# A gated block with attention on one core: features in rows for the last layer, the output projection and the result; statistics in pairs at the start; the last gates computed in one step with their scale

## The chip, the cores and the metric

The kernel runs on one core of a Trainium2 chip. The metric is device time in microseconds of one execution. The core has five engines that run their own queues of instructions in order: TensorE (PE, with its weight loads shown apart as PEld), VectorE (DVE), ScalarE (ACT), GpSimd (POOL) and SyncE (SP, which here only issues DMAs). They meet through semaphores. TensorE writes to PSUM, which this kernel divides into eight banks of 128 x 512 float32.

## The reference

Eight sequences of 512 tokens with 256 features, all float32. A layer norm feeds two branches, whose product is added to the input:

```python
x = L0_attn_query                      # (8, 512, 256)
xn = _layernorm(x, axis=-1)
s = _L0_attn_ref(xn, in_proj_w, out_proj_w)   # 16 heads of 16, rope, causal window of 250
g = _silu(_L0_ffn_ref(xn, k0, k1, k2, s0, s1, s2))
x = x + s * g
return x
```

The feed-forward branch has three layers (512 to 1024, 1024 to 1024, 1024 to 256), the first of which sees `[xn, -xn]`. Its kernels are boolean and stand for +1 and -1; each layer has one scale, and the first two end in `2 * relu`.

## The kernel before

**Precision.** Activations of the feed-forward branch are split into a float16 high part and a rest that is fed as fp32r; both are multiplied with the same +1/-1 weights, kept in both types (`w0`, `w1`, `w2` with `h` and `l`). So each product of this branch is a pass over `h` and a pass over `l`, summed in one PSUM bank. The attention's projections are float32.

**Stages of a batch b.** `stats` and `norm` make xn with tokens in rows; `turn_x` transposes it on PE (`xnT_ps`, L268) into `xT` (features in rows), and into its high and low parts. `project` makes the two halves `a` and `b` (the two members of each rope pair) of k and of q: DVE multiplies each with cos and sin (`m_ka`, `m_kb`, `m_qa`, `m_qb`, L319), POOL adds (`rotate`, L339), ACT and DVE split the result (`split_hi` L356, `split_lo` L363), and it goes through DRAM into stacks of four heads. `project_v` makes v. `layer` (L415) makes `h1` (eight tiles of 128 features by 512 tokens) and `h2` (eight more); after each, ACT writes the high part (L426) and DVE the low part (L424). `last` makes z, the third layer, and the gate: before, with **tokens** in rows, 128 tokens by 256 features per tile `t` of four: the stationary operand is a piece of h2, the moving one is w2. `gate_ready` makes silu out of it: exp on ACT (L496), plus one on POOL (L499), reciprocal on DVE (L503), and a product on POOL (L504). Attention goes in nine score steps per batch (`step`): scores (L605), exp (L624), masks on POOL (L640, L647), values (L679), `keep` (L699, L703), and the division by the sums (`invert`, `divide`). `project_o` (L782) multiplies with w_o, again 128 tokens by 256 features per tile; DVE multiplies with the gate (L804), POOL adds the residual, which `project_o` has loaded from `x` again (L787, L809), and SP stores (L810).

**What sets the order.** The order on all five queues is written by a planner in the code. Each piece has a due place (`at`) and a PE cost; pieces are sorted by `at`, their costs add up to a clock, and a piece may name follow-up work with a delay on that clock. A batch has `SEQ = 42` units of `at`; `last_at` places the z of batch b among the h1 tiles of batch b+1, `late` places its output projections. Score steps are put before those pieces that are in `quick`, evenly by cost. Batch 0 starts at -40: loads, statistics, transposes, `warm` blocks (matmuls of the identity), the weights (`make_w0`, `make_w1`, on DVE, ACT and POOL), then k, q, h1 and v. In the last batch layer 2 runs in two halves of 256 tokens; z of tiles 0 and 1 follows the first half (`how == "soon"`), z of tiles 2 and 3 the second (`"final"`).

**Buffers.** PSUM: two tiles of two banks for scores (`ps_s`), one bank for the values (`ps_o`), three single banks (`ps_m`, tag `mm`) for everything else: transposes, projections, h, z, output projection. `m_*b` has one buffer, so the rope products of q's b half wait for k's rotation. SBUF tags that matter here: `gate0` to `gate3` (single), `den` and `xr` (two each, 128 x 256), `xn` (two).

**Loads at the start.** SP issues x tiles 0 and 1, k0, rope, k2, w_o; ACT issues x tiles 2 and 3, the scales, w_qkv (one load, L124) and k1 (L127).

Of the kernel before, what the change touches and what calls it, by code (L numbers as in the profile page):

```python
# [21 lines left out]
EPS = 1e-5  # L22
# [12 lines left out]
def tile_attention_times_gated_ffn(  # L35
    ctx: ExitStack,
    tc: tile.TileContext,
    x: bass.AP,
    w_qkv: bass.AP,
# [6 lines left out]
    out: bass.AP,  # L46
):

# [75 lines left out]
    nc.scalar.dma_start(wqkv_sb, w_qkv.rearrange("(c p) f -> p c f", p=P))  # L124
# [44 lines left out]
    def make_w0(c):  # L169

        nc.vector.tensor_tensor(w0["h"][:, c], kb0[:, c], kb0[:, EC + c], ALU.subtract)
        nc.scalar.copy(w0["l"][:, c], w0["h"][:, c])
# [58 lines left out]
    def stats(b):  # L231
        st = states[b] = {}
        mv = small.tile([P, NT, 2], F32, tag="mv", name=f"mv_{b}")
        rstd = small.tile([P, NT], F32, tag="rstd", name=f"rstd_{b}")
        for t in range(NT):
            bn = small.tile([P, 6], F32, tag="bn", name=f"bn_{b}_{t}")
            nc.vector.bn_stats(bn, xs[b, t])
            nc.vector.bn_aggr(mv[:, t, :], bn)
        nc.vector.tensor_scalar(rstd, mv[:, :, 1], EPS, None, ALU.add)
        nc.gpsimd.tensor_tensor(rstd, rstd, minus_half, ALU.pow)  # L240
        nc.vector.scalar_tensor_tensor(
            mv[:, :, 1], mv[:, :, 1], LEAST_VAR, ones, ALU.is_ge, ALU.mult,
            accum_out=counts[:, 2 * B + b : 2 * B + b + 1],
        )
        st["mv"], st["rstd"] = mv, rstd
# [9 lines left out]
    def turn_x(b, t, plain=False):  # L255
# [10 lines left out]
        pt = ps_m.tile([P, EC, P], F32, tag="mm", name=f"xnT_ps_{b}_{t}")  # L266
# [7 lines left out]

        def parts_():
            xT = st["xT"][:, :, ts(t, P)]
            if b == 0:
                nc.scalar.copy(xT, pt)
            else:
                nc.vector.tensor_copy(xT, pt)  # L280
            nc.scalar.mul(hi, pt, sgnx)
# [3 lines left out]

        return [(0.0, parts_), (0.5, low)]

# [14 lines left out]
    def project(b, what, part):  # L302
        st = states[b]
        col = E * "qk".index(what) + P * "ab".index(part)
        ps = ps_m.tile([P, T], F32, tag="mm", name=f"{what}{part}_ps_{b}")
# [11 lines left out]

        def times(i):
            nc.vector.tensor_tensor(  # L319
                m[:, i], ps, rope_sb[:, i if part == "a" else 1 - i], ALU.mult  # L320
            )

        def both():
            times(0)
            times(1)
            if part == "b":
                return [
                    (1.4, lambda: rotate(b, what)),
                    (4.0 if b else 7.0, lambda: split_hi(b, what)),
                    (5.1 if b else 8.2, lambda: split_lo(b, what)),  # L330
                ]

        return [(0.0, both)]
# [95 lines left out]
    def last(b, t, how):  # L429
        st = states[b]  # L430
        pz = ps_m.tile([P, E], F32, tag="mm", name=f"z_ps_{b}_{t}")
        if how == "at once":
            for c in range(NF1):
                nc.tensor.matmul(
                    pz, st["h2p"][:, c, ts(t, P)], w2["l"][:, c].bitcast(F32),
                    start=(c == 0), stop=(c == NF1 - 1),
                )
        else:
            for p in "hl":
                for c in range(NF1):  # L440
                    nc.tensor.matmul(  # L441
                        pz, st["h2" + p][:, c, ts(t, P)], w2[p][:, c],
                        start=(c == 0 and p == "h"), stop=(c == NF1 - 1 and p == "l"),
                    )
        gate = st["gate", t] = outs.tile([P, E], F32, tag=f"gate{t}", name=f"gate_{b}_{t}")
        if how == "final":
            den = denominator(b, t)

            def ends():
                nc.scalar.activation(den, pz, AF.Exp, scale=scales[:, 1:2])  # L450
                nc.vector.tensor_scalar(gate, pz, scales[:, 0:1], None, ALU.mult)
                return [(0.3, add)]

            def add():
                nc.scalar.activation(den, den, AF.Identity, bias=1.0)
                return [(0.3, invert_)]

            def invert_():
                nc.vector.reciprocal(den, den)
                if t + 1 < NT:  # L460
                    nc.gpsimd.tensor_tensor(gate, gate, den, ALU.mult)
                st["den"] = den
# [3 lines left out]
        def scale():  # L466
            nc.vector.tensor_scalar(gate, pz, scales[:, 0:1], None, ALU.mult)
            if how != "later":
                return [(0.5 if t == 0 else 4.5, lambda: gate_ready(b, t))]
# [20 lines left out]
    def denominator(b, t):  # L490
        return work.tile([P, E], F32, tag="den", name=f"den_{b}_{t}")

    def gate_ready(b, t):
        st = states[b]
        gate, den = st["gate", t], denominator(b, t)
        nc.scalar.activation(den, gate, AF.Exp, scale=-1.0)  # L496

        def add():
            nc.gpsimd.tensor_scalar(den, den, 1.0, None, ALU.add)  # L499
            return [(0.9, invert_)]  # L500

        def invert_():
            nc.vector.reciprocal(den, den)  # L503
            return [(1.8, lambda: nc.gpsimd.tensor_tensor(gate, gate, den, ALU.mult))]  # L504
# [7 lines left out]
    def last_at(b, t):  # L512

        if b + 1 < B:
            return SEQ * (b + 1) + 2 * L1 * (t + 1) + L3 * t
        half = t // 2
        return SEQ * b + NF0 * L1 + NT * L3 + HALF * (half + 1) - 2 * L3 + L3 * (t % 2)

    def late(b, t):

        if b + 1 == B and t >= NT // 2:
            return last_at(b, NT - 1) + L3 + 0.9 * (t - NT // 2)
        if b + 1 == B:
            return SEQ * b + 40.0 + 0.9 * t
        return SEQ * (b + 1) + (32.0 + 3.2 * t if b + 2 < B else 18.0 + 2.5 * t)

    def finish_ffn(b, t, how):
        quick.add(last_at(b, t))
        out = [(last_at(b, t), L3, lambda: last(b, t, how))]
        if how == "later":  # L530
            out.append((late(b, t) - 4.0, 0, lambda: gate_ready(b, t)))
        return out

    def ffn(b):
# [3 lines left out]
        for f in range(NF0):  # L538
# [3 lines left out]
            if f % 2 and b > 0:  # L542
                now += L3
# [234 lines left out]
    def project_o(b, t, final=False):  # L778
        st = states[b]
        pp = ps_m.tile([P, E], F32, tag="mm", name=f"att_ps_{b}_{t}")  # L780
        for c in range(EC):
            nc.tensor.matmul(  # L782
                pp, st["V", c][:, ts(t, P)], wo_sb[:, c, :],
                start=(c == 0), stop=(c == EC - 1),
            )
        xr = work.tile([P, E], F32, tag="xr", name=f"xr_{b}_{t}")
        nc.sync.dma_start(xr, x[b, ts(t, P), :])  # L787
        st["xr", t] = xr
        if final and t + 1 == NT:
            att = work.tile([P, E], F32, tag="xn", name=f"att_{b}_{t}")  # L790

            def out_of_psum():
                y, den = st["gate", t], st["den"]
                nc.scalar.copy(att, pp)
                nc.gpsimd.tensor_tensor(y, y, att, ALU.mult)
                nc.vector.tensor_tensor(y, y, den, ALU.mult)
                nc.vector.tensor_tensor(y, y, xr, ALU.add)
                nc.sync.dma_start(out[b, ts(t, P), :], y)
# [3 lines left out]
        def product():  # L802
            y = st["gate", t]
            nc.vector.tensor_tensor(y, pp, y, ALU.mult)  # L804
            return [(1.0 if final else 0.5, store)]

        def store():
            y = st.pop(("gate", t))
            nc.gpsimd.tensor_tensor(y, y, xr, ALU.add)  # L809
            nc.sync.dma_start(out[b, ts(t, P), :], y)  # L810
# [3 lines left out]
    def finish(b, final=False):  # L814
        out = []
        for t in range(NT):
            end = final and t >= NT // 2
            out.append((late(b, t), 0.87, lambda t=t, end=end: project_o(b, t, end)))
# [25 lines left out]
    def swap():  # L844
# [5 lines left out]
        (-38.5, 0, signs), (-40.5, 0, lambda: warm(12)), (-34.5, 0, lambda: warm(3)),  # L850
        (-32.5, 0, lambda: warm(5)),
        (19.2, 0, make_w2), (22.5, 0, swap), (SEQ * (B - 1) + 45.0, 0, add_up),
    ]
    for c in range(EC):
        everything.append((-30 + 0.1 * c, 0, lambda c=c: make_w0(c)))
# [9 lines left out]
    for b in range(B):  # L865
        everything += prepare(b) + ffn(b)
        for t in range(NT):
            how = "later" if b + 1 < B else "soon" if t < NT // 2 else "final"
            everything += finish_ffn(b, t, how)
# [59 lines left out]
    with tc.If(found < n_rows):  # L929
        for b in range(B):  # L930
# [4 lines left out]
            for t in range(NT):  # L935
                run(finish_ffn(b, t, "at once"))
# [67 lines left out]
```

## Time and profile before

| | us |
|---|---|
| median of three runs | 627.94 (627.25 to 629.54) |
| profiled execution, its time | 628.36 |
| its span, first to last instruction | 626.6 |
| PE busy | 608.6 |
| DVE busy | 394.1 |
| POOL busy | 316.2 |
| ACT busy | 299.7 |

The span lies 1.8 us inside the time of the same execution. Busy times of engines overlap. A line of the timeline has the start (us from the span's start), the duration of the merged group, the engine, the line of the kernel, the operation, the tiles written and read, the shapes, the count, and in brackets the idle time of the engine just before it with what ended it. A line of the list of waits has the waiting engine, tile and line, what it waited for, the microseconds in total, the number of times and the longest. Groups by line and shape that come up later:

```
L424 DVE h2l   512 columns x56: 680 ns     256 columns x16: 398 ns
L426 ACT h1h   512 columns: 597 ns         L496 ACT exp, 256 columns: 409 ns
L499 POOL +1   256 columns: 852 ns         L767 POOL tensor_scalar, 512 columns: 1499 ns
L503 DVE reciprocal, 256 columns: 1752 ns  L754 DVE reciprocal, 128 columns: 933 ns
L504 POOL product, 256 columns: 755 ns     L763 POOL product, 512 columns: 1285 ns
L804 DVE product out of PSUM, 256 columns: 403 ns
L809 POOL add of the residual, 256 columns: 810 ns
```

DMA issues to landing: w_qkv 8.0 us (768 KB), k0 8.2 (512 KB), rope 9.9 (512 KB), k1 11.3 (1024 KB, landed at 15.04), residual 2.8 (128 KB), store of the result 1.7 (128 KB).

### The profile page before, as it was taken

What the parts mean: (1) busy time and instruction counts of PE and PEld (TensorE: products, weight loads), DVE (VectorE), ACT (ScalarE), POOL (GpSimd) and SP (SyncE); (2) the same over time, 40 slices, a digit from 0 to 9 for tenths busy, and PEclk for the clock granted to TensorE, in tenths of its full rate; (3) what the DMA queues carried; (4) which work ended last, traced back from release to release, by engine and by line L of the source; (5) the groups of instructions that cost most, each with busy time, mean ns of one, the idle gap of its engine ahead of it and who ended that gap; (6) DMA issues with size and microseconds to landing.
All of it is one profiled execution on the core that took longest, in us unless ns stands there. A gap on an engine that the chain in (4) does not pass through costs nothing.

```text
span 626.6 us, 12051 instructions
## 1 busy us (share of the span) xinstructions
PE 608.6 (97%) x4842; PEld 398.4 (64%) x4842; DVE 394.1 (63%) x667; ACT 299.7 (48%) x441; POOL 316.2 (50%) x409
## 2 busy tenths in 40 slices
PE   8899999999999999999999999999999999999994
PEld 6455576556665567655676566765676556767793
DVE  6773535667575774766658576485665668456573
ACT  4566655534554445545354454453444544564411
POOL 2954542456533655427634366235662356638641
PEclk9999999999999999999999999999999999999998
DMA  9352721116311263114421252412532116230101
GB/s 273 117 197 95 260 85 51 51 68 216 122 51 51 87 208 110 52 51 172 139 93 51 75 214 76 143 33 86 208 94 88 51 69 227 77 109 19 53 18 48
DMA packets 38193, 67.20 MB, mean 107 GB/s; under 512 B 5104, under 2 KB 19184, under 8 KB 38128
## 3 DMA queue, kind: packets, MB, share of 16 engines
q1 hardware_dynamic: 36384, 64.24, 30.5%
q10 hardware_dynamic: 1744, 2.10, 1.0%
q8 instruction: 40, 0.66, 0.4%
q14 instruction: 25, 0.20, 0.1%
HBM read 36.96 MB, written 29.36 MB: 106 GB/s over the span
## 4 chain that ended last, share of the span: by engine, by line
PE 85%; DVE 5%; POOL 3%; DMA 3%; ACT 2%; issue 1%; SPq 0%; POOLq 0%; ACTq 0%; DVEq 0%
PE h_ps L415 41%; PE po L679 11%; PE z_ps L441 9%; PE sc L605 8%; PE v_ps L292 4%; PE att_ps L782 4%; PE qa_ps L307 2%; PE kb_ps L307 2%; PE qb_ps L307 2%; DMA kb<-in_k_dram 2%; PE ka_ps L307 2%; PE xnT_ps L268 1%; DVE den L503 1%; DVE h2l L424 1%; DVE xn L250 1%
## 5 line engine op out<-in xcount | busy, mean ns | idle before, releaser
L624 ACT ACTIVATE p<-sc 128x1024 f32<-128x1024 f32 (+2 forms) x144 | 138.5, 1013 | 75.0 <-PE sc L605 41.0
L415 PE MATMUL h_ps<-h1l,w1l_sb 128*128 128x512 f32 (+1 forms) x576 | 144.2, 392 | 0.0
L640 POOL TENSOR_SCALAR_AFFINE_SELECT p<-p 128x512 f32<-128x512 f32 x128 | 90.3, 711 | 104.0 <-ACT p L624 104.0
L415 PE MATMUL h_ps<-h1h,w1h_sb 128*128 128x512 f16 (+1 forms) x576 | 123.0, 356 | 0.5 <-ACT v_pad L299 0.5
L415 PEld LDWEIGHTS h_ps<-h1l,w1l_sb 128*128 128x128 f32 x576 | 99.5, 188 | 25.7 <-issue 6.8
L426 ACT ACTIVATE h2h<-h_ps 128x512 f16<-128x512 f32 (+1 forms) x72 | 39.6, 550 | 140.3 <-PE h_ps L415 140.2
L415 PEld LDWEIGHTS <-w1h_sb 128*128 128x128 f16 x576 | 51.5, 98 | 55.1 <-issue 13.4
L679 PE MATMUL po<-p,v_pad 128*32 128x378 f32 (+4 forms) x1216 | 77.2, 372 | 1.3 <-DVE S L703 1.1
L647 POOL TENSOR_SCALAR_AFFINE_SELECT p<-p 128x512 f32<-128x512 f32 (+1 forms) x96 | 50.0, 521 | 54.6 <-ACT p L624 49.7
L424 DVE SCALAR_TENSOR_TENSOR h2l<-h_ps,h2h 128x512 fp32r<-128x512 f32 (+1 forms) x72 | 44.3, 617 | 48.5 <-ACT h2h L426 48.5
L503 DVE RECIPROCAL den<-den 128x256 f32<-128x256 f32 x30 | 52.5, 1752 | 28.2 <-POOL den L499 28.1
L424 DVE SCALAR_TENSOR_TENSOR h1l<-h_ps,h1h 128x512 fp32r<-128x512 f32 x64 | 42.4, 675 | 34.8 <-ACT h1h L426 34.8
L605 PEld LDWEIGHTS sc<-q,k 32*128 32x128 f32 x1216 | 44.1, 184 | 26.1 <-issue 15.0
L754 DVE RECIPROCAL S<-S 128x128 f32<-128x128 f32 x64 | 58.9, 933 | 0.0
L426 ACT ACTIVATE h1h<-h_ps 128x512 f16<-128x512 f32 x64 | 38.2, 597 | 41.8 <-PE h_ps L415 41.2
L605 PE MATMUL sc<-q,k 32*128 32x378 f32 (+4 forms) x1216 | 57.2, 306 | 0.0
L415 PE MATMUL h_ps<-xl,w0l_sb 128*128 128x512 f32 x128 | 52.5, 491 | 0.0
L679 PEld LDWEIGHTS po<-p,v_pad 128*32 128x32 f32 x1216 | 31.3, 109 | 30.8 <-issue 16.2
L809 POOL TENSOR_TENSOR gate<-gate,xr 128x256 f32<-128x256 f32 x31 | 25.1, 810 | 46.8 <-DMA xr<-in_x_dram 41.2
L441 PE MATMUL z_ps<-w2l_sb,h2l 128*128 128x256 f32 x256 | 38.3, 291 | 0.4 <-DVE h2l L424 0.4
L415 PE MATMUL h_ps<-xh,w0h_sb 128*128 128x512 f16 x128 | 38.6, 383 | 0.0
L339 POOL TENSOR_TENSOR m_ka<-m_ka,m_kb 128x512 f32<-128x512 f32 x16 | 20.1, 1278 | 30.3 <-DVE m_kb L319 30.3
(97 smaller groups left out, 811.0 us busy)
## 6 DMA issues: line engine op xcount, KB each, us to landing
q<-dq SPq DMA_DIRECT2D x64, 256.0 KB, 3.6
dq<-qh SPq DMA_DIRECT2D x16, 512.0 KB, 3.4
dq<-m_qa SPq DMA_DIRECT2D x16, 512.0 KB, 5.0
k<-dk SPq DMA_DIRECT2D x32, 256.0 KB, 2.8
dk<-kh SPq DMA_DIRECT2D x8, 512.0 KB, 2.6
dk<-m_ka SPq DMA_DIRECT2D x8, 512.0 KB, 2.6
xr<-in_x_dram SPq DMA_DIRECT2D x32, 128.0 KB, 2.8
out_dram<-gate SPq DMA_DIRECT2D x32, 128.0 KB, 1.7
```

Of the source, the lines that this page charges most:

```text
L307: nc.tensor.matmul(ps, wqkv_sb[:, c, ds(col, P)], st["xT"][:, c, :], start=(c == 0), stop=(c == EC - 1),)
L415: nc.tensor.matmul(ph, w[p][:, c, ts(f, P)], st[src + p][:, c, cols], start=(k == 0), stop=(k == n - 1),)
L424: nc.vector.scalar_tensor_tensor(lo, ph, 0.0, hi, ALU.max, ALU.subtract)
L426: high = lambda: nc.scalar.activation(hi, ph, AF.Relu)
L441: nc.tensor.matmul(pz, st["h2" + p][:, c, ts(t, P)], w2[p][:, c], start=(c == 0 and p == "h"), stop=(c == NF1 - 1 and p == "l"),)
L503: nc.vector.reciprocal(den, den)
L605: nc.tensor.matmul(sc[r // 2][:, r % 2, ds(off, n)], st["k0", g][row, ts(j, P)], st[f"q{turn}", g][row, ds(j * P + first, n)], start=(turn ...
L624: nc.scalar.activation(p[:, 2 * half : 2 * half + 2, :n], sc[half][:, :, :n], AF.Exp, scale=D ** -0.5,)
L640: nc.gpsimd.affine_select(out=block, in_=block, compare_op=ALU.is_ge, fill=0.0, base=0, pattern=[[0, 4], [1, P]], channel_multiplier=-1,)
L647: nc.gpsimd.affine_select(out=block, in_=block, compare_op=ALU.is_ge, fill=0.0, base=-1, pattern=[[0, 4], [-1, beyond]], channel_multiplier=1,
L679: nc.tensor.matmul(po[32 * r : 32 * r + 32, ds(j * P + first, n)], v_columns(j, g, r), p_[:, r, ds(off, n)], start=(j == 0), stop=(done an ...
L754: nc.vector.reciprocal(part, part)
```

## The change

1. **Features in rows.** `last`, `project_o` and the result are turned: w2 and w_o are now the stationary operands, h2 and V the moving ones. A batch's z has two units `u` of 128 features by 512 tokens instead of four tiles of 128 tokens by 256 features; in the last batch four units of 128 features by 256 tokens. The residual comes from a transposed copy of x, the result is written transposed (`x_t`, `out_t`), and both are laid out on the host. `residual` is issued in `gate_ready` or `last`, ahead of the projection, not in it. `den` and `xr` are single buffers (`beside`). The reciprocal of `gate_ready` is cut into two halves. Places change (`last_at`, `late`): z comes after the fourth and the eighth tile of h1, not after every second.
2. **The start.** w_qkv is loaded in three parts, k's first. The deviations of batch 0 are made in pairs of tiles. Transposes of tiles 0 and 1 and the projections of q use the score pool. The high and low parts of x come after all four copies. `w0h` of the first half is placed ahead of them on DVE. The `warm` blocks are 9, 2 and 1 matmuls, where they were 12, 3 and 5. The products of q's b half come 1.5 units later.
3. **The last batch.** All four projections come after the last z, whose banks are from the score pool. The gate of the last two units is one operation, z times scale times reciprocal, and the last store is issued by ACT.

```diff
-    nc.scalar.dma_start(wqkv_sb, w_qkv.rearrange("(c p) f -> p c f", p=P))
+    for n in (1, 0, 2):
+        nc.scalar.dma_start(
+            wqkv_sb[:, :, ts(n, E)], w_qkv[:, ts(n, E)].rearrange("(c p) f -> p c f", p=P)
+        )
...
+            if (t + 1) % n == 0:
+                part = rstd[:, t + 1 - n : t + 1]
+                nc.vector.tensor_scalar(part, mv[:, t + 1 - n : t + 1, 1], EPS, None, ALU.add)
+                nc.gpsimd.tensor_tensor(part, part, minus_half[:, :n], ALU.pow)
...
+        if b == 0:
+
+            nc.scalar.copy(xT, pt)
+            st["parts", t] = [high, low]
+            if t + 1 == NT:
+                first_parts(2, 3)
+            return
...
+        if b == 0 and what == "q":
+            ps = ps_s.tile([P, 2, T], F32, tag="sc", name=f"{what}{part}_ps_{b}")[:, 0]
...
-        return [(0.0, both)]
+
+        return [(1.5 if b == 0 and what + part == "qb" else 0.0, both)]
...
+    def outputs(b):
+
+        n = 1 if b + 1 < B else 2
+        return [(f, ts(half, T // n)) for half in range(n) for f in range(EC)]
...
+    def residual(b, u):
+        f, cols = outputs(b)[u]
+        xr = states[b]["xr", u] = beside(b, u, "xr")
+        nc.sync.dma_start(xr, x_t[b, ts(f, P), cols])
...
-                        pz, st["h2" + p][:, c, ts(t, P)], w2[p][:, c],
+                        pz, w2[p][:, c, ts(f, P)], st["h2" + p][:, c, cols],
...
+                nc.scalar.activation(den, den, AF.Identity, bias=1.0)
+                return [(0.0 if u == 2 else 0.88, ready)]
...
+            def ready():
                 nc.vector.reciprocal(den, den)
-                if t + 1 < NT:
-                    nc.gpsimd.tensor_tensor(gate, gate, den, ALU.mult)
-                st["den"] = den
+                nc.vector.scalar_tensor_tensor(
+                    gate, pz, scales[:, 0:1], den, ALU.mult, ALU.mult
+                )
...
+            return [(0.9 + 1.1 * k, lambda k=k: invert_(k)) for k in range(2)]
...
         if b + 1 < B:
-            return SEQ * (b + 1) + 2 * L1 * (t + 1) + L3 * t
+            return SEQ * (b + 1) + 4 * L1 * (u + 1) + 2 * L3 * u
...
         if b + 1 == B:
-            return SEQ * b + 40.0 + 0.9 * t
-        return SEQ * (b + 1) + (32.0 + 3.2 * t if b + 2 < B else 18.0 + 2.5 * t)
+            return last_at(b, 3) + L3 + 0.9 * u
+        return SEQ * (b + 1) + (33.5 + 6.4 * u if b + 2 < B else 19.2 + 5.0 * u)
...
-                pp, st["V", c][:, ts(t, P)], wo_sb[:, c, :],
+                pp, wo_sb[:, c, ts(f, P)], st["V", c][:, cols],
...
+            very_last = final and u + 1 == len(outputs(b))
+            adder, queue = (nc.vector, nc.scalar) if very_last else (nc.gpsimd, nc.sync)
+            adder.tensor_tensor(y, y, xr, ALU.add)
+            queue.dma_start(out_t[b, ts(f, P), cols], y)
...
-        (-38.5, 0, signs), (-40.5, 0, lambda: warm(12)), (-34.5, 0, lambda: warm(3)),
-        (-32.5, 0, lambda: warm(5)),
+        (-34.6, 0, signs), (-40.5, 0, lambda: warm(9)), (-34.7, 0, lambda: warm(2)),
+        (-32.5, 0, lambda: warm(1)), (-31.0, 0, lambda: enough(0)),
+        (-32.7, 0, lambda: first_parts(0, 1)),
...
-        everything.append((-30 + 0.1 * c, 0, lambda c=c: make_w0(c)))
+        everything += [
+            (-34.4 if c == 0 else -32.8, 0, lambda c=c: make_w0h(c)),
+            (-32.9 if c == 0 else -32.6, 0, lambda c=c: make_w0l(c)),
+        ]
```

## The prediction

> **What bounds the kernel now.** I read the stretch-by-stretch busy times first, because the page's averages (PE 97%, DVE 63%) mix stages with different limits:
>
> ```profile
> core 0: us, PE busy (x) PEld busy (x) DVE busy (x) ACT busy (x) POOL busy (x), PEclk, DMA share, GB/s
> 0.00:11.00 11.00, 8.00 (x48) 7.48 (x49) 6.49 (x24) 3.95 (x9) 3.12 (x10) 1.00 0.82 253
> 11.00:18.00 7.00, 7.00 (x19) 2.93 (x18) 6.01 (x10) 4.46 (x4) 2.77 (x3) 1.00 0.82 240
> 18.00:34.00 16.00, 12.65 (x53) 7.45 (x52) 11.88 (x24) 8.87 (x15) 14.63 (x11) 1.00 0.37 145
> ...
> 116.00:190.00 74.00, 73.89 (x581) 47.30 (x579) 47.97 (x80) 34.62 (x51) 37.24 (x49) 1.00 0.32 108
> ...
> 560.00:616.00 56.00, 54.48 (x548) 45.85 (x541) 34.59 (x60) 19.82 (x37) 31.40 (x40) 1.00 0.16 48
> 616.00:626.60 10.60, 1.46 (x7) 0.95 (x5) 4.09 (x6) 1.10 (x3) 2.29 (x3) 0.76 0.12 34
> ```
>
> The reader should see that the middle is PE alone (73.89 of 74 us), so nothing done there to another engine shortens the kernel. Time can be won before 34 us, in the last batch, and after its last matmul. The timeline of the start says what PE waits for there:
>
> ```profile
> 6.26 1.05 POOL L240 TENSOR_TENSOR rstd<-rstd,minus_half 128x4 f32<-128x4 f32 x1 [3.56 <-DVE rstd L239]
> 7.35 0.73 DVE L250 TENSOR_SCALAR xn<-x,mv,rstd 128x256 f32<-128x256 f32 x2 [0.17 <-POOL rstd L240]
> ...
> 15.23 2.38 POOL L180 TENSOR_SCALAR w1l_sb<-kb,sgn,sgnn 128x1024 fp32r<-128x1024 uint8 x2 [7.92 <-DMA kb<-in_k_dram]
> ...
> 17.57 2.51 POOL L339 TENSOR_TENSOR m_ka<-m_ka,m_kb 128x512 f32<-128x512 f32 x2
> ...
> 20.12 1.29 DVE L319 TENSOR_TENSOR m_qb<-qb_ps,rope_sb 128x512 f32<-128x512 f32 x2 [2.18 <-POOL m_ka L339]
> ...
> 21.46 1.13 PE L292 MATMUL v_ps<-wqkv_sb,xT 128*128 128x256 f32 x4 [1.32 <-DVE m_qb L319]
> ```
>
> A chain runs from a load (k1, landed at 15.04) over two weight conversions on POOL and the rotation of k to the rope product of q (DVE, 20.12), and from there to PE. Further PE waits of 0.76, 0.80 and 0.46 us follow at 27.85, 31.60 and 33.19. In the list of waits two lines concern what the change enlarges or moves:
>
> ```profile
> POOL gate L809 <- DMA xr<-in_x_dram: 41.2, 19, 3.4
> ...
> DVE den L503 <- POOL den L499: 28.1, 24, 2.5
> ```
>
> The first is the residual, loaded only when it is wanted; the second is DVE held at a reciprocal until POOL has added 1. Neither shows as PE time in the middle. Last I read the tail, after the last matmul:
>
> ```profile
> 616.92 1.74 DVE L459 RECIPROCAL den<-den 128x256 f32<-128x256 f32 x1
> ...
> 618.86 0.41 DVE L796 TENSOR_TENSOR gate<-gate,den 128x256 f32<-128x256 f32 x1
> ...
> 619.30 0.83 DVE L797 TENSOR_TENSOR gate<-gate,xr 128x256 f32<-128x256 f32 x1
> 620.16 0.35 SPq L798 DMA_DIRECT2D out_dram<-gate  x1
> 620.61 1.14 SPq L810 DMA_DIRECT2D out_dram<-gate  x1
> ```
>
> [...] (1) [...] 16 matmuls of z (256 columns) take 1.83 us in the chain of waits, 16 of layer 2 (512 columns) 3.6 to 3.8. (2) [...] DVE stood 2.18 us before m_qb, with h1l, whose input was ready, behind it. (3) [...] the h2l operation takes 398 ns at 256 columns and 680 at 512.
>
> **The change, part by part.** All sums are made against the profiled execution: span 626.6, time 628.36, which is 0.42 above the median of 627.94.
>
> *Features in rows, middle of the kernel.* Per batch z goes from 64 matmuls of 256 columns to 32 of 512, the output projection from 16 instructions to 8. Columns are the same; [...] and over seven batches **-0.7** (bounds -1.2 and +0.5: the chain's rows do not separate 2 x 1.83 from 3.6 to 3.8). DVE, ACT and POOL get fewer, larger pieces: POOL goes from 4 x (0.85 + 0.75 + 0.81) = 9.6 us per batch to about 2 x (1.5 + 1.28 + 1.28) = 8.1 (512-column rows of L767 and L763). PE's queue covers this, so I cost it at nothing. The residual is issued 4.5 planner units before its use instead of beside it, so the 41.2 us of POOL waits go; PE did not see them, so they are worth nothing either. Its buffer is now single, so on SP the second residual load waits for the first half's final add; behind it stand k/q stores and loads, for which the old store waited the same way. The per-gate chain becomes longer: exp 0.6, add 1.5, two reciprocals 3.5, product 1.3 = 6.9 us, where it was 0.41 + 0.85 + 1.75 + 0.75 = 3.8. The plan leaves it 4.5 units and the projection's 1.75, plus a score step if one falls in between. DVE will therefore sometimes stand before the product. I place z, v and h1 of the next batch by hand on the three PSUM buffers: h1l of the first tile frees its bank about 3.5 us after that tile began, the third h1 wants one at 3.6. This just fits: 0; if it slips, it is the slower rival.
>
> *The start.* x's deviations in pairs: pow runs at about 5.2 and 6.45 instead of once at 6.26; the first normalization comes at 6.35, not 7.35, the third at 7.5. Four copies on ACT (0.38 each), now without the f16 parts between them, end near 9.2, and the last warm block is one matmul, not five. w_qkv was one load, landed at about 10.2 (8.0 us from issue); its k third is now first, by my estimate from 253 GB/s there by 7. So ka starts at 9.25, not 11.06. But this is not the gain. On DVE w0h0 now stands ahead of all four xl, waits for k0 (landed about 9.9), and DVE then has 2 x 1.2 + 4 x 0.45 + 0.25 to do before m_ka: 14.4 instead of 13.16; m_kb ends at 17.0. The rotation of k cannot start before 15.04 + 0.2 + 2.38 = 17.6 in either kernel. Three ACT issues of about 0.5 us stand where one was, ahead of k1's, so k1 may land 0 to 1 us later. What does gain: q's banks come from the score pool, free when xl of tiles 0 and 1 are done (13.7 and 14.1), so qa, qb, h1_0, h1_1, v0 run 13.75, 15.5, 17.2, 18.1, 19.0, and h1l0 (19.0) passes ahead of m_qb, which still waits until 20.1. At 21.4 PE has v0 and h1_2 done, where v0 just started before. h1l1 and h1l2 follow m_qb, so the low part of k starts at 22.8, not 25.09, and the rest of the DVE queue (h1l3 to h1l7, statistics of batch 1) moves up by the same 2.3: layer 2 starts at about 30.9, not 33.19. I take **-2.0** (bounds -3.0 and -0.5: each 0.1 us of k1 delay costs 0.1).
>
> *The last batch, before its end.* PE waits 1.11 us at 572.99 for keep (DVE), behind the reciprocal of batch 6's gate, and 0.41 at 592.03, where z waits for h2l behind a count. In the new order that h2l precedes the count (0.41 goes), and the first wait keeps most of its length, since the two half reciprocals and the 1.5 us add take its place. **-0.5** (bounds -1.2 and +0.5).
>
> *The tail.* All four projections come after the last z, so z ends 2 x 0.86 = 1.72 us sooner (614.0, not 615.74) and PE ends where it did. DVE then decides: reciprocal of gate 2 at 613.25 to 615.0, joined gate 0.45, product 0 0.41, reciprocal of gate 3 615.95 to 617.7, joined gate to 618.15, the add of output 1 to 618.6, product 3 to 619.0, last add 0.41 to 0.83: the last store is issued at 619.5 to 619.9, now on ACT, where it was 620.61 on SP. **-0.9** (bounds -1.3 and 0). The price is DVE order: without the joined gate two more DVE operations would stand here.
>
> Sum: -0.7 - 2.0 - 0.5 - 0.9 = -4.1; 628.36 - 4.1 = 624.3, or **623.8** against the median.
>
> **Rivals.** *The start stays pinned to k1.* If k1 lands 1 us later, or m_kb is pushed past it (0.6 us of slack), the start gives 0.8, z nothing, the last batch 0.3, the tail 0.7: -1.8, 626.1. For it: POOL idled 7.92 us for that load, and "k sooner" does not touch it. Against: the bytes ahead of k1 are the same.
>
> *Bursts of h1.* Four tiles of h1 now come together between the z blocks, with ACT 0.60 and DVE 0.69 for each 0.91 of PE, and three v beside them. A loss of 0.4 per batch in seven batches gives -4.1 + 2.8 = -1.3, 626.6. Against: PE idles only 0.1 us per batch there now.
>
> *The wide gate chain (slower).* At the border of two batches DVE holds, in order, the second product, h2l, two keeps, count and h1l0. If the gate is over 0.5 us later than I placed it, every later one of these slips and PE waits for a bank. A slip of 1.2 us beyond that in seven batches is +8.4, in all +4.3: 632.2. For it: 28.1 us of DVE waits on the same add, soon 1.5 us long instead of 0.85, and a chain of 6.9 us in some 6.3 to 8. Against: those waits cost PE nothing now, and POOL has 1.5 us less to do per batch and no residual to wait for.
>
> **Chances.** About 0.5% (3.1 us) is what a measurement of this kernel can tell from no change. Forecast 0.64 (0.58 of it beyond 0.5%), k1 0.17 (0.02 beyond), bursts 0.09 (none), gate chain 0.10 (0.09 slower by over 0.5%). Faster 0.60, same 0.31, slower 0.09. The range, 621.5 to 627.5, takes the start's and tail's outer bounds and both middle cases, and leaves out the gate chain and the extremes.
>
> **What would show it.** Right: ka at about 9.3, the rotation of k still at 17.6, low k near 22.8, layer 2 near 31; 73.9 of 74 us of PE busy in the middle and a batch period not longer than the present 75; the last store issued 0.7 to 1.1 us sooner relative to the end of PE. Wrong: k1 landing after 15.5, PE waiting at the head of a batch for h1l or the product, or a last reciprocal that starts after 616.5 on the shifted scale.

## The result and the profile after

The changed kernel takes 623.75 us (median of five runs, 621.87 to 624.11), the kernel before, measured beside it, 628.63 (627.25 to 629.54): a ratio of 0.9916, 95% interval 0.99 to 0.9931. The forecast was 623.8. Its parts, however, were not of the sizes forecast. This table is read from the two profiled executions:

| us | before | after | difference |
|---|---|---|---|
| k1 landed | 15.04 | 15.43 | +0.39 |
| layer 2 of batch 0 starts | 33.19 | 32.36 | -0.83 |
| first h1 of batch 1 | 87.99 | 87.17 | -0.82 |
| batch period, mean of six (first h1 of batch 1 to that of batch 7) | 74.985 | 74.630 | -0.355, six times: -2.13 |
| last batch: its first h1 to the end of PE | 79.56 | 78.61 | -0.95 |
| end of PE to the end of the span | 9.10 | 7.50 | -1.60 |
| span | 626.56 | 621.05 | -5.51 |
| time of that execution | 628.36 | 623.75 | -4.61 |

What lies outside the span grew from 1.8 to 2.7 us in these two executions (1.9 to 2.3 in the other four of the changed kernel), so the spans differ by more than the times. The stretch-by-stretch busy times of the changed kernel (start and end, length, then busy time and count of PE, PEld, DVE, ACT and POOL, the granted clock, the DMA share and rate):

```profile
9.00:18.00 9.00, 8.75 (x24) 4.21 (x25) 7.45 (x14) 6.31 (x10) 2.39 (x3) 1.00 0.86 262
18.00:31.00 13.00, 9.15 (x38) 5.37 (x37) 10.99 (x21) 7.40 (x13) 12.80 (x11) 1.00 0.40 157
116.00:190.00 74.00, 73.95 (x543) 44.16 (x542) 46.91 (x76) 35.64 (x50) 35.57 (x44) 1.00 0.32 107
558.00:614.00 56.00, 54.32 (x546) 44.41 (x542) 36.44 (x60) 20.96 (x38) 30.34 (x35) 1.00 0.15 45
614.00:621.10 7.10, 0.00 (x0) 0.00 (x0) 1.33 (x4) 0.00 (x0) 1.00 (x2) 0.83 0.23 73
```

The middle is PE alone, as before (73.95 of 74 us, with 543 matmuls in place of 581). The stretch from 18 to 31 us is still not: PE idles 3.9 of 13 us while POOL is full. The timeline of the start says why:

```profile
15.61 2.38 POOL L188 TENSOR_SCALAR w1l_sb<-kb,sgn,sgnn 128x1024 fp32r<-128x1024 uint8 x2 [8.44 <-DMA kb<-in_k_dram]
...
17.95 2.50 POOL L381 TENSOR_TENSOR m_ka<-m_ka,m_kb 128x512 f32<-128x512 f32 x2
...
20.49 1.29 DVE L360 TENSOR_TENSOR m_qb<-qb_ps,rope_sb 128x512 f32<-128x512 f32 x2 [1.47 <-POOL m_ka L381]
...
22.43 1.13 PE L328 MATMUL v_ps<-wqkv_sb,xT 128*128 128x256 f32 x4 [1.38 <-DVE h1l L466]
...
22.78 2.50 POOL L381 TENSOR_TENSOR m_qa<-m_qa,m_qb 128x512 f32<-128x512 f32 x2
22.90 3.47 DVE L405 TENSOR_TENSOR m_ka<-m_ka,kh 128x1024 fp32r<-128x1024 f32 x1
...
27.02 1.13 PE L328 MATMUL v_ps<-wqkv_sb,xT 128*128 128x256 f32 x4 [1.64 <-DVE h1l L466]
...
29.94 0.16 DVE L260 SCALAR_TENSOR_TENSOR mv<-mv,ones 128x4 f32<-128x4 f32 x1
...
32.36 1.89 PE L457 MATMUL h_ps<-h1h,w1h_sb 128*128 128x512 f16 x8 [0.46 <-ACT v_pad L335]
```

The chain of before is whole: k1, two conversions, k's rotation, q's rope product. Low k (`m_ka<-m_ka,kh`, the low part of k) starts at 22.90 instead of 25.09, but lasts 3.47 us instead of 2.11, beside POOL's rotation of q: it ends at 26.36, only 0.83 sooner. From there DVE's queue runs as before, and layer 2 follows 5.99 us later in both kernels, so this 0.83 is what layer 2 gained. In the list of waits (us in total, times, longest) these lines stand in the place of the two that the prediction named:

```profile
DVE den L572 <- POOL den L567: 25.2, 15, 2.9
...
POOL gate L882 <- DVE gate L875: 12.1, 9, 4.9
...
POOL gate L574 <- DMA xr<-in_x_t_dram: 11.1, 4, 2.8
```

The wait for the added 1 was 28.1 us (24 times). The add of the residual (now L882) waited 41.2 us for its load; it now waits for DVE's product alone. The 11.1 us that are still put down to that load stand before the gate's product (L574), which does not read it. PE waits for none of them in the middle. The timeline after the last matmul, which ends at 613.55:

```profile
611.91 1.74 DVE L528 RECIPROCAL den<-den 128x256 f32<-128x256 f32 x1
...
613.68 0.48 DVE L529 SCALAR_TENSOR_TENSOR gate<-z_ps,scales,den 128x256 f32<-128x256 f32 x1
614.08 0.41 DVE L868 TENSOR_TENSOR gate<-gate,xr 128x256 f32<-128x256 f32 x1
...
614.42 0.41 DVE L875 TENSOR_TENSOR gate<-att_ps,gate 128x256 f32<-128x256 f32 x1
...
614.87 0.50 DVE L882 TENSOR_TENSOR gate<-gate,xr 128x256 f32<-128x256 f32 x1
615.40 0.37 ACTq L883 DMA_DIRECT2D out_dram<-gate  x1
```

The last store is issued 1.85 us after the end of PE, where it was 3.15 (620.61 against 617.46). The other 0.3 us of the tail lies between issue and the end of the span; it is not to be read, since from the end of PE to the end of the span it was 7.0 to 7.5 us in the runs below that leave the tail as it is.

### The profile page after: what moved, and what is told of

The parts are those of the page before. It is cut to its first block, busy times and chain, and to the rows that moved or that the text cites. A ratio compares the mean times of both kernels' runs of the same rounds, so it can differ in the third digit from the quotient of the medians.

```text
span 621.1 us, 11288 instructions
## 1 busy us (share of the span) xinstructions
PE 604.3 (97%) x4546; PEld 372.5 (60%) x4546; DVE 382.9 (62%) x641; ACT 299.7 (48%) x428; POOL 308.1 (50%) x367
## 4 chain that ended last, share of the span: by engine, by line
PE 90%; DVE 3%; DMA 2%; POOL 2%; ACT 1%; issue 0%; ACTq 0%; POOLq 0%; DVEq 0%
PE h_ps L457 45%; PE po L746 11%; PE z_ps L511 9%; PE sc L672 8%; PE v_ps L328 4%; PE att_ps L853 4%; PE qa_ps L346 2%; PE kb_ps L346 2%; PE qb_ps L346 2%; DMA kb<-in_k_dram 2%; PE ka_ps L346 2%; PE xnT_ps L291 1%; ACT p L691 1%; DVE den L528 1%; DVE m_ka L405 1%; DMA x<-in_x_dram 1%
## 5 line engine op out<-in xcount | busy, mean ns | idle before, releaser
L707 POOL TENSOR_SCALAR_AFFINE_SELECT p<-p 128x512 f32<-128x512 f32 x128 | 92.3, 727 | 133.6 <-ACT p L691 133.5
L572 DVE RECIPROCAL den<-den 128x256 f32<-128x256 f32 (+1 forms) x32 | 52.6, 1645 | 25.2 <-POOL den L567 25.2
L672 PEld LDWEIGHTS sc<-q,k 32*128 32x128 f32 x1216 | 44.0, 184 | 28.1 <-issue 20.4
L821 DVE RECIPROCAL S<-S 128x128 f32<-128x128 f32 x64 | 57.4, 919 | 0.0
L328 PE MATMUL v_ps<-wqkv_sb,xT 128*128 128x256 f32 x128 | 33.1, 381 | 3.8 <-DVE h1l L466 3.8
L511 PE MATMUL z_ps<-h2l,w2l_sb 128*128 128x512 f32 (+1 forms) x144 | 35.8, 390 | 0.0
```

The costliest lines, as they stand in the source:

```text
L328: nc.tensor.matmul(v.rearrange("p n s d -> p (n s d)"), st["xT"][:, c, ts(t, P)], wqkv_sb[:, c, 2 * E :], start=(c == 0), stop=(c == EC - 1),)
L511: nc.tensor.matmul(pz, w2[p][:, c, ts(f, P)], st["h2" + p][:, c, cols], start=(c == 0 and p == "h"), stop=(c == NF1 - 1 and p == "l"),)
L572: nc.vector.reciprocal(part, part)
L672: nc.tensor.matmul(sc[r // 2][:, r % 2, ds(off, n)], st["k0", g][row, ts(j, P)], st[f"q{turn}", g][row, ds(j * P + first, n)], start=(turn ...
L707: nc.gpsimd.affine_select(out=block, in_=block, compare_op=ALU.is_ge, fill=0.0, base=0, pattern=[[0, 4], [1, P]], channel_multiplier=-1,)
L821: nc.vector.reciprocal(part, part)
```

## Experiments on the start

In the texts on record "A" and "B" are the theories named there. All experiments but two (w1l behind k's rotation, q's rotation sooner) are one execution each. Over all these measurements the kernel before ran from 626.6 to 630.0 us, so a single time says little, and they are read in their traces. The changed kernel was run once more beside the second set:

> The changed kernel once more, beside the versions of this call: about 623.8 us. Layer 2 of batch 0 starts 16.9 to 17.0 us after k1 has landed, wherever between 13.8 and 15.9 that is; the batch period is 74.63.

It took 623.5 us (ratio 0.9925, interval 0.9908 to 0.9941), with a period of 74.630 and layer 2 at 16.99 us after k1. That distance is the measure of the start used below, because k1's landing moves by itself: from 13.8 to 16.1 us over all these runs. It was 18.15 in the kernel before and 16.93 in the first run of the changed one: a gain of 1.2 us at equal k1.

**One load of w_qkv** (the three-part loop back to one load):

```diff
-    for n in (1, 0, 2):
-        nc.scalar.dma_start(wqkv_sb[:, :, ts(n, E)], ...)
+    nc.scalar.dma_start(wqkv_sb, w_qkv.rearrange("(c p) f -> p c f", p=P))
```

> w_qkv is one load again. Theory A (k's projection is not what the start waits for; k1 is, and it landed at 15.04 when w_qkv was one load, 15.43 with three): the projection of k starts about 1 us later than 9.25, near 10.3, but k1 lands near 15.0 and layer 2 starts 0.2 to 0.5 us before 32.36. Theory B (the start is worth what k's projection is): layer 2 starts about 1 us after 32.36.

The time was 623.90. k's projection started at 10.82 instead of 9.25, m_kb ended at 17.08 instead of 15.25, and layer 2 came 16.96 us after k1: no change. k1 did not land sooner (15.79), as A had asked, nor did layer 2 come 1 us later, as B had. "k sooner" is worth nothing while k's rotation stands behind k1's conversions on POOL.

**w1l behind k's rotation** (two conversions moved in POOL's order):

```diff
-        ("l", 0, -20, nc.gpsimd), ("l", 1, -19, nc.gpsimd),
+        ("l", 0, 4.8, nc.gpsimd), ("l", 1, 4.9, nc.gpsimd),
```

> The first two fp32r weight tiles of layer 2 are converted on POOL after the rotation of k, not before it. Theory A (the start is pinned to the load of k1, because the conversions that wait for it stand ahead of k's rotation on POOL): the rotation of k starts at about 15.3, right after m_kb, instead of 17.95; m_qb at about 17.9 instead of 20.49; layer 2 starts 1.5 to 2.6 us before 32.36, and the time falls by as much. Theory B (DVE's own amount of work sets the start): the rotation comes sooner, but layer 2 starts within 0.5 us of 32.36.

622.23 us (621.66 to 623.24), ratio to the kernel before 0.9899, interval 0.9878 to 0.992. The timeline of this kernel:

```profile
14.42 2.51 POOL L381 TENSOR_TENSOR m_ka<-m_ka,m_kb 128x512 f32<-128x512 f32 x2 [7.25 <-DVE m_kb L360]
...
18.22 1.28 DVE L360 TENSOR_TENSOR m_qb<-qb_ps,rope_sb 128x512 f32<-128x512 f32 x2
...
21.22 1.51 DVE L405 TENSOR_TENSOR m_ka<-m_ka,kh 128x1024 fp32r<-128x1024 f32 x1 [0.24 <-ACT kh L398]
...
21.61 3.48 POOL L381 TENSOR_TENSOR m_qa<-m_qa,m_qb 128x512 f32<-128x512 f32 x2
...
29.72 1.89 PE L457 MATMUL h_ps<-h1h,w1h_sb 128*128 128x512 f16 x8 [0.46 <-ACT v_pad L335]
...
30.82 3.69 DVE L268 TENSOR_SCALAR xn<-x,mv,rstd 128x256 f32<-128x256 f32 x2
...
36.36 0.89 PE L291 MATMUL xnT_ps<-ident,xn 128*128 128x128 f32 x4 [0.96 <-DVE h2l L466]
```

POOL now waits for m_kb, not for the load; m_qb no longer waits at all, and layer 2 starts 2.6 us sooner, or 2.3 counted from k's projection, which by itself came 0.34 sooner here (8.91). 1.2 us are given back by batch 1 (its first h1 at 85.70 against 87.17): DVE takes 3.69 us for two normalizations that take 0.40 each when alone and took 2.68 together in the changed kernel, beside POOL's conversions of w2, and PE waits 0.96 us. So the start was pinned by POOL's order: the two conversions ahead of k's rotation.

**q's rotation sooner too** (beside that, w1l 2 and w1h 2 from 5.1 and 5.2 to 9.3 and 9.4):

> Beside the two w1l conversions that already stand behind k's rotation, the two conversions at 5.1 and 5.2 (w1l 2, w1h 2) go to 9.3 and 9.4, so POOL comes to q's rotation first. Theory A (the start is a chain over POOL whose order decides): q's rotation starts at about 19.5 instead of 21.61, the low parts of q at about 26 to 27 instead of 28.00, layer 2 of batch 0 up to 1 us sooner than 29.72; some of it is given back at the start of batch 1, as w2 comes later; the span ends 0 to 1 us below the version with two moved conversions (619.4), that is 622 us or a little less, and 1.5 to 2.5 us under the changed kernel. Rival B (with k out of the way the start is bound by TensorE's own work and by DVE, not by POOL): layer 2 stays within 0.3 us of 29.7 counted from the same work, the time within 0.5 us of 622.2; DVE's low k beside POOL's rotation of q takes some 3.5 us again instead of 1.5.

622.44 us (ratio 0.9913, interval 0.9896 to 0.9931). q's rotation did move, to 19.54, but q's low parts stayed at 28.28, because DVE's written order reaches them only then; layer 2 was at 30.00. Theory A fell: once k is out of the way, q's rotation is not the bound. Rival B was right in this, but its sign, low k of 3.5 us, did not come (1.64). Measured beside each other, this kernel's span was 619.5 and the changed one's 620.7. Moving the conversions gains about 1 us, at the edge of what these intervals separate.

**q's rotation later**, to take it from beside low k:

```diff
-            (1.4, lambda: rotate(b, what))
+            (4.7 if b == 0 and what == "q" else 1.4, lambda: rotate(b, what))
```

> The rotation of q on POOL comes one weight conversion later, so that the low part of k on DVE does not run beside it. Theory A ([...] which made the low part of k 3.47 us long where it was 2.11 before): the low part of k takes 2.0 to 2.4 us, and layer 2 starts about 1 us before 32.36. Theory B (the low part of k is long for another reason): it stays over 3 us and layer 2 starts at 32.4 or later.

624.46 us. Low k took 2.17 us as expected, but layer 2 came 17.07 us after k1, no sooner (0.46 of that is a slower clock of PE in the last v, 1.59 us instead of 1.13, with 0.82 granted from 30 to 32 us; see the last section). Two other runs, in which only the middle or the very end was edited, showed the same thing unasked: there low k took 2.21 and 2.25, and layer 2 came 16.64 and 16.67 us after k1. The timeline of one of them (the last store by SP, below):

```profile
22.32 3.49 POOL L381 TENSOR_TENSOR m_qa<-m_qa,m_qb 128x512 f32<-128x512 f32 x2
22.43 2.25 DVE L405 TENSOR_TENSOR m_ka<-m_ka,kh 128x1024 fp32r<-128x1024 f32 x1
...
25.79 3.56 POOL L188 TENSOR_SCALAR w1l_sb<-kb,sgn,sgnn 128x1024 fp32r<-128x1024 uint8 x3
...
28.24 1.11 DVE L260 SCALAR_TENSOR_TENSOR mv<-mv,ones 128x4 f32<-128x4 f32 x1
...
30.02 1.13 PE L328 MATMUL v_ps<-wqkv_sb,xT 128*128 128x256 f32 x4 [1.75 <-DVE h1l L466]
```

Low k, one operation of DVE, takes 1.23 us with POOL idle (in batch 1); q's rotation is two operations of POOL of 1.28 us each. In the changed kernel low k starts at 22.90, beside them, and ends at 26.36, 1.08 us after the second of them (25.28). Here low k ends at 24.67, and the second operation of POOL is the long one: it ends at 25.81, 1.14 us later. So in both traces the one that ends last does so by its own length after the other, within 0.15 us, as if it had waited. One pair does not show it: in the changed kernel q's low part starts at 30.63 beside POOL's `pow` for batch 1 (profiled from 29.99 to 31.01), and still takes 1.22.

Behind both operations of POOL low k takes some 1.25 us more (3.47, not 2.21 or 2.25), yet without that layer 2 comes only 0.3 sooner. The trace shows where the rest goes. DVE now comes to the check of batch 1's variances (L260, 128 x 4 values) while POOL is still at its w1l conversions, and the check takes 1.11 us instead of 0.16: it ends within 0.02 us of the end of a conversion (29.35). It took 1.04 to 1.13 us in five runs (this one, z in halves, q's rotation later, and the two with moved conversions), each time ending so. From the end of low k to layer 2 those five needed 6.87 to 6.99 us (7.45 with the slower clock), and 5.99 to 6.00 in the eight runs, the kernel before among them, in which it took 0.16 at the same place in DVE's order. So one long DVE operation is traded for another, and one of 512 values takes back most of the gain. Moving this check was not tried.

**q's b half at once** (its delay of 1.5 units away):

```diff
-        return [(1.5 if b == 0 and what + part == "qb" else 0.0, both)]
+        return [(0.0, both)]
```

> The products of q's b half are planned at once again, ahead of the low part of the first tile of h1 on DVE, as they were before the change. Theory A (the passing of h1's low part is what let PE go on during the wait for k's rotation): PE waits at the first v or the third tile of h1 for 1 to 2 us more, but since the low part of k starts at about the same time, layer 2 starts 0.3 to 1.5 us after 32.36. Theory B (the passing is worth nothing because the queue behind is bound by the rotation): layer 2 within 0.2 us of 32.36.

629.86 us, beside 629.04 for the kernel before: without this delay nothing of the change's gain is left. Its timeline:

```profile
20.95 1.29 DVE L360 TENSOR_TENSOR m_qb<-qb_ps,rope_sb 128x512 f32<-128x512 f32 x2 [4.37 <-POOL m_ka L381]
...
22.89 1.01 PE L457 MATMUL h_ps<-xh,w0h_sb 128*128 128x512 f16 x2 [3.33 <-DVE h1l L466]
...
31.42 0.59 PE L457 MATMUL h_ps<-xh,w0h_sb 128*128 128x512 f16 x2 [1.62 <-ACT v_pad L335]
...
35.69 1.70 PE L328 MATMUL v_ps<-wqkv_sb,xT 128*128 128x256 f32 x4 [2.29 <-DVE h1l L466]
```

DVE stands 4.37 us before m_qb, with h1l, ready and wanted, behind it; PE waits 3.33 us for that h1l and later twice more. Layer 2 came 21.3 us after k1, 4.3 later than in the changed kernel, where 0.3 to 1.5 was expected. Part of it is PE's own clock, which was granted at 0.61 and 0.53 from 22 to 26 us.

## Experiments on the middle

All of these are read by the batch period. It was 74.630 in both runs of the changed kernel, and 74.631 to 74.644 in six of the seven others whose middle is the same; the seventh, with one load of w_qkv, had 74.690, since one of its six batches took 74.91. In the two experiments on z and in that with four units every one of the six batches is longer than in the changed kernel.

**z in halves** (each z matmul of 512 columns as two of 256, interleaved; z's values come out different in this form, but the matmuls, their sizes and their places are the intended ones), and **z in two groups** (the loop over halves outermost):

```diff
-                        pz, w2[p][:, c, ts(f, P)], st["h2" + p][:, c, cols],
+                        pz[:, ts(k, T // 2)], w2[p][:, c, ts(f, P)],
+                        st["h2" + p][:, c, ts(k, T // 2)],
```

> In batches 0 to 6 every matmul of z is two of 256 columns, one right after the other with the same weights; places, groups and all other engines stay. The distance from batch to batch is 74.63 us in the changed kernel and 74.97 before. Theory A (the middle gained because there are fewer instructions): the distance grows by 0.08 us or more, up to 0.2. Theory B (it gained because there are fewer boundaries between groups on PE[...]): it stays within 0.04 us of 74.63.

> In batches 0 to 6 z is made in two groups of 16 matmuls of 256 columns, one after the other, so that the number of matmuls is the same as in the kernel with halves, and one more change from fp32r back to float16 is in each block. Theory A (instructions): the same as the kernel with halves. Theory B (boundaries): 0.04 to 0.2 us per batch more than 74.63, and more than the kernel with halves by at least 0.03.

Periods 74.698 and 74.745 (times 623.05 and 623.77). 32 more instructions cost 0.07 us, 2.1 ns each, between the 0.08 of theory A and the 0.04 of B. A second group at each of the two places adds 0.048, as theory B of the second text asked.

**Output projection in two groups** (the same edit in `project_o`):

> In batches 0 to 6 the output projection is made in halves of 256 columns, one group after the other in the same place. Theory A (instructions): about 0.02 us per batch more than 74.63. Theory B (the gain of the projection lies in being put into layer 2 twice per batch, not four times): within 0.02 us of 74.63, so the boundary count and not the size counts.

Period 74.673, +0.043: twice what A gave, and not B. Together these account for 0.16 of the 0.355 us per batch.

**Four units of 256 columns in every batch**:

```diff
-        n = 1 if b + 1 < B else 2
+        n = 2
...
-            return SEQ * (b + 1) + 4 * L1 * (u + 1) + 2 * L3 * u
+            return SEQ * (b + 1) + 2 * L1 * (u + 1) + L3 * u
```

(`late`, `finish_ffn`, `ffn` and the buffers of `beside` follow.)

> Features stay in rows, but every batch has four units of 256 columns (64 z and 16 projection matmuls in four groups each, at four places a batch, as the kernel before had them in its orientation), not two of 512. Theory A (the middle's gain is fewer instructions and fewer groups at fewer places on TensorE; the orientation itself gives nothing): the period of the middle batches goes back to 74.9 to 75.0 us, the time to about 626. Rival B (the gain beyond the 0.16 us that halving matmuls and groups measured lies in the orientation, that is in where weights and data sit): the period stays at 74.75 to 74.8.

Period 74.862, between the two: theory A asked for 74.9 to 75.0, B for 74.75 to 74.8. Time from each matmul's start to the next one's start, summed by output, mean of batches 2 to 5:

| us per batch | before | four units | changed |
|---|---|---|---|
| z | 7.407 (x64) | 7.393 (x64) | 7.306 (x32) |
| output projection | 3.261 (x16) | 3.263 (x16) | 3.031 (x8) |
| h2 | 30.455 | 30.460 | 30.611 |
| v | 3.583 | 3.542 | 3.445 |
| po | 9.013 | 8.960 | 8.958 |

By periods, halving the units is worth 0.232 of the 0.355: 0.158 for instructions and groups, and 0.074, by difference, for there being fewer places. The other 0.123 came with the turned operands, but also with what else the change holds in the middle (the residual issued sooner, the reciprocal in two halves, other buffers); these were not separated, and four units were run once. The table also warns: the projection gains 0.23 and its neighbour h2 loses 0.16, so one row alone misleads. The row of v is such a case, as its own instructions are the same. A row takes in the time up to whatever comes next. In the kernel before, each batch had one v matmul ahead of a score (0.309 us to the next start, where 0.216 is usual) and one ahead of z (0.253 on average); in the changed kernel all stand ahead of v or h1, at 0.216. That is 0.13 of v's 0.138: new neighbours, not a faster v. Why po falls is not settled.

## Experiments on the tail

**Gate and scale apart** (for the last two units):

```diff
+                nc.vector.tensor_scalar(gate, pz, scales[:, 0:1], None, ALU.mult)
...
-                nc.vector.scalar_tensor_tensor(
-                    gate, pz, scales[:, 0:1], den, ALU.mult, ALU.mult
-                )
+                nc.vector.tensor_tensor(gate, gate, den, ALU.mult)
```

> The last two gates are made in two operations again, z times scale on DVE while ScalarE makes the denominator, then times the reciprocal. From the end of PE to the issue of the last store it was 1.85 us in the changed kernel and 3.15 before. Theory A (the tail is DVE's own work after the last z, so each operation counts): the last store is issued 0.3 to 0.5 us later relative to the end of PE. Theory B (the first operation hides while DVE waits for the denominator, so joining is worth nothing): within 0.15 us of 1.85.

625.41 us; the last store was issued 2.91 us after the end of PE (613.04), 1.06 later than in the changed kernel, twice what theory A gave. Its timeline:

```profile
610.66 0.43 DVE L530 TENSOR_TENSOR gate<-gate,den 128x256 f32<-128x256 f32 x1
...
611.73 1.74 DVE L529 RECIPROCAL den<-den 128x256 f32<-128x256 f32 x1
...
612.58 1.40 POOL L865 TENSOR_TENSOR gate<-gate,att 128x256 f32<-128x256 f32 x2
...
613.51 0.76 DVE L530 TENSOR_TENSOR gate<-gate,den 128x256 f32<-128x256 f32 x1
...
614.06 0.78 POOL L867 TENSOR_TENSOR gate<-gate,xr 128x256 f32<-128x256 f32 x1
614.19 0.94 DVE L867 TENSOR_TENSOR gate<-gate,xr 128x256 f32<-128x256 f32 x1
...
615.95 0.37 ACTq L882 DMA_DIRECT2D out_dram<-gate  x1
```

The reciprocal starts 0.33 us later against the end of PE: that is the instruction saved. The product, which now reads two operands from SBUF, takes 0.76 where the joined form, with one in PSUM, takes 0.48 in the changed kernel, beside the same two products of POOL (612.75 to 614.16), and where the same product took 0.43 for the unit before, with POOL idle (610.66). It ends 0.29 us after POOL's two products (613.98). The add is 0.94 instead of 0.41: its start falls 0.13 after POOL's add has started, and it too ends 0.29 after that one (614.84). Both end after POOL's operation by their own length (0.43 and 0.41), within 0.15 us, as low k did. The join is worth three times the instruction that it saves.

**Last store by SP**:

```diff
-            adder, queue = (nc.vector, nc.scalar) if very_last else (nc.gpsimd, nc.sync)
+            adder, queue = (nc.vector, nc.sync) if very_last else (nc.gpsimd, nc.sync)
```

> The last store of all is issued by SP, behind the three other stores of the last batch, instead of by ACT. Theory A (the own queue is part of the tail's gain): SP issues the two stores before it at 0.59 us from each other and comes to the last one about 0.6 us after the third, where ACT issued it 0.29 after; the last store goes out 2.1 to 2.2 us after the last matmul instead of 1.84 to 1.85, and the span ends later by up to as much. Rival B (the gain is the gate's chain alone, the queue is free by then): 1.8 to 1.9 us after the last matmul, the tail unchanged.

The last store was issued at 616.86, 2.28 us after the end of PE (614.58), +0.43: theory A, with a little more than its size. The data were ready at 616.39, as early against PE as before. The time, 624.35, is not to be read for this edit, as the start lost some 1.35 us by itself (last section).

## Why the prediction was right, and where it was not

- *The total* (623.8 against 623.75) is right by luck. The parts sum to -5.5 us of the span, where -4.1 was forecast: the start gave 1.2 less, the middle 1.4, the last batch 0.45 and the tail 0.7 more. The time of that execution fell by only 4.6, as 0.9 us came in outside the span, and the forecast had taken off a further 0.42 for the median. Against the 628.63 of the kernel before when measured beside it, the changed one is 4.9 us faster, not 4.1.
- *The start* was forecast at -2.0 and measured -0.83 (-1.2 at equal k1), inside its bounds. ka (9.25), k's rotation behind k1's conversions, h1l0 ahead of m_qb and low k's start (22.8; measured 22.90) came as written. The step that failed is "the rest of the DVE queue ... moves up by the same 2.3: layer 2 starts at about 30.9": it took each DVE operation at the length that it had before. Moving low k forward set it beside q's rotation on POOL, and it took 3.47 us instead of 2.11; that 1.36 is the part of the 2.19 by which it began sooner that layer 2 did not get. Where low k was shorter (2.21 and 2.25 us; layer 2 at 16.64 and 16.67 after k1, not 16.93), the check of batch 1's variances was long in its place (1.04 to 1.13 us, not 0.16). The rival of k1 pinning the start had the right mechanism, as the moved conversions unpinned it, but neither of the causes that it named came: k1 landed 0.39 later, not 1, and m_kb ended at 15.25, ahead of k1. (17.0 was written; k0 landed at 8.60, not 9.9, so this part of the DVE queue ran ahead of the forecast, for nothing.) One reading under (2) is too strong: in the kernel before, h1l's input was ready only at 19.86, so it stood ready for 0.26 of the 2.18 us.
- *The middle* was forecast at -0.7, an estimate of the author's, and measured -2.13, beyond its bound of -1.2. At the price measured here (0.07 us for 32 matmuls) 40 fewer instructions are only about 0.09 of 0.355. Left out was what a group and a place cost PE, and what came with the turned operands. "This just fits: 0" for the three PSUM buffers held: PE waits for neither gate nor bank, so bursts and the wide gate chain did not come.
- *The last batch* was forecast at -0.5 and measured -0.95. The wait of 0.41 went and the one of 1.11 stayed (1.23), as written. But the first was worth more than its idle time: start to start, the sixteen z matmuls around it took 2.61 us and now 1.92, 0.69 less. The projections gave 0.21, po 0.19, h1 0.12 and batch 6's z in fewer pieces only 0.03, against 0.10 more in scores (with the wait of 1.23) and 0.21 in h2.
- *The tail* was forecast at -0.9 and measured -1.60, of which 1.30 is the last store's issue, where 0.7 to 1.1 was written; the bound was -1.3. The join, priced as two DVE operations, measured 1.06, because without it two DVE operations also took longer beside POOL's (0.76 us, not 0.48, and 0.94, not 0.41); the queue measured 0.43 by itself. The two overlap.

## What to carry to other kernels

When a queue is reordered, look up what runs on DVE and POOL at the new place: here low k, moved beside POOL's rotation of q, took 3.47 us instead of 2.11, and a check of 128 x 4 values beside POOL's conversions 1.11 instead of 0.16, which took back most of what the moves gained. Before pulling a stage forward, find what its consumer waits for last; here k's projection came 1.6 us sooner (9.25 instead of 10.82) for nothing, and the order of two weight conversions decided. On a kernel bound by PE, halving the number of groups and their places can bring more than the per-instruction price: here 0.232 us per batch, where 40 instructions at the measured price are about 0.09.

## What the runs showed that was not expected

Short waits of PE in the start were followed by a granted clock of 0.50. Busy times in four stretches of the kernel with the last store by SP, same columns as above:

```profile
28.00:30.00 2.00, 0.28 (x2) 0.00 (x0) 1.93 (x6) 0.60 (x1) 2.00 (x3) 1.00 1.00 395
30.00:32.00 2.00, 1.52 (x6) 0.88 (x7) 2.00 (x3) 0.81 (x2) 2.00 (x2) 0.91 0.23 90
32.00:34.00 2.00, 2.00 (x6) 0.75 (x5) 2.00 (x3) 0.70 (x1) 2.00 (x2) 0.50 1.02 403
34.00:36.00 2.00, 2.00 (x8) 1.34 (x7) 0.90 (x1) 0.00 (x0) 2.00 (x3) 0.74 0.99 292
```

From 32 to 34 us PE is busy all the time with 6 matmuls, where the changed kernel has a clock of 1.00 until after its last matmul. Layer 2 of batch 0 started 0.3 us sooner after k1, and batch 1 came 1.35 later (73.15 us after k1, not 71.80). It happened in four of the runs: this one, z in halves, q's rotation later and q's b half at once (twice).

The traces record when the granted clock changes. Each stretch at half clock in the start lasts 3.413 us, and the stretches at full clock are whole multiples of it (10.24, 13.65, 23.89 us: 3, 4 and 7; 614.399 us in the profiled execution of before and 610.986 in that of the changed kernel: 180 and 179). So each trace can be laid out in windows of that length, counted from its own changes, and PE's busy time summed over each:

| window before a drop | ends at, us | PE busy of 3.41 us |
|---|---|---|
| q's b half at once | 22.46 | 0.51 |
| q's b half at once | 36.11 | 1.12 |
| last store by SP | 31.64 | 1.21 |
| z in halves | 30.75 | 1.43 |
| q's rotation later | 31.27 | 1.76 |

In none of these was PE wholly idle. Over all runs, every window at full clock with at most 1.43 us busy was followed by a drop and none with 1.80 or more; between them, seven from 1.62 to 1.78 were not and the one of 1.76 was. So in these traces what parts the two lies between 1.43 and 1.80 us, no closer. A wait that falls across the border of two windows is shared by them: with q's rotation sooner, PE waited 1.68 and 0.46 us, but its two windows were busy 2.37 and 2.32 us, and the clock stayed at 1.00. The changed kernel itself, with 1.78 in one window of its start, kept 1.00 too.
